# Recommendation kernel: a tile's gathers split by partitions, a token of three tiles fetched row by row, seven token buffers

## The chip, the cores and the metric

The kernel runs on one core of a Trainium2 chip. The metric is device time in microseconds of that core; lower is better. Before the change the median of three runs is 7685.06 us (7660.61 to 7702.07).

## The reference

A batch of 16384 examples goes through embedding look-ups and a small network:

```python
tok = word_emb[token_idx].mean(axis=1)          # 32 tokens of 300 values, table of 50000 rows
e1, e2, e3 = means of 20 rows of 64 values each, tables of 1000, 5000 and 10000 rows
o1, o2, o3, o4 = one row of 64 values each, tables of 100, 50, 20 and 1000 rows
emb = concatenate([tok, e1, e2, e3, o1, o2, o3, o4], axis=1)       # 748 values
wide = sums of the same look-ups in tables of one column
h = relu(emb @ W1 + b1); h = relu(h @ W2 + b2); h = relu(h @ W3 + b3)   # 1024, 512, 256
return sigmoid(h @ Wd + bd + wide)
```

All of it is in float32. The 32 token look-ups are far the largest part of the data: 16384 x 32 rows of 1200 bytes, 629 MB.

## The kernel before

The batch is cut into 128 tiles of 128 examples, one example per partition. Indices come in blocks of four tiles (`load_indices`, L266), the network runs on blocks of two tiles, 256 examples (`mlp`, L474).

Each tile goes through two separate paths.

- The small tables stay on the chip. For each tile VectorE makes one-hot rows (`one_hots`, L322), TensorE multiplies them into counts (`counts`, L340), ScalarE evicts the counts from the one `pc` buffer (L347), and TensorE multiplies counts by table rows (`small_sums`, L365). This is done in 11 steps to a tile.
- The 32 token rows of each example are gathered from HBM by GpSimd (`tokens`, L245): one indirect DMA per token and tile, 128 rows of 1200 bytes each (L255), 4096 in all. Two tokens make a group with one buffer, `tok_rows`; there are 16 groups to a tile and eight buffers (`TOK_BUFS`). VectorE adds a group into a running sum in PSUM (`add_up`, L237 to L243) three groups after its gathers were issued in the program's order (`TOK_LAG`). A gather waits for the add that read its buffer eight groups before.

Then both are transposed (L405 to L431) and the network follows: matmuls in `layer` (L461), evictions with relu by ScalarE (L470), the last sum (L490), the sigmoid (L491) and the store of 256 results by SyncE (L493). The tiles `h1` and `h3` of the network have one buffer between them: the first eviction of the next block overwrites what the store reads.

The order of the work is written out by hand. One loop of 1424 steps (L570; 128 tiles of 11 steps and 16 more) issues for each step its one-hots and counts, then as many token groups as keep pace with the steps (`toks.to`, L608: 2051 calls over 1424 steps), then small sums, then matmuls of the network. `Paced` (L496) runs a generator until it has done a given amount. Each engine works through its own instructions in this order. GpSimd's queue holds little but gathers. SyncE's queue holds the loads of indices, tables and weights, and the stores; each transfer that SyncE issues uses one of eight semaphores in turn, and waits for the transfer before on that semaphore.

Of the kernel before, what the change touches and what calls it, by code (L numbers as in the profile page):

```python
# [8 lines left out]
F32 = mybir.dt.float32  # L9
BF16 = mybir.dt.bfloat16  # L10
FP8 = mybir.dt.float8e3
I32 = mybir.dt.int32
U32 = mybir.dt.uint32
# [4 lines left out]
P = 128  # L18
N_TOK, TOK_D = 32, 300
# [2 lines left out]
D1, D2, D3 = 1024, 512, 256  # L22
TOK_GROUP = 2
TOK_LAG = 3
TOK_BUFS = 8
WAKE = 16
EARLY = 3
BLOCK = 512
# [6 lines left out]
STEPS = -(-HALF // ONEHOT)  # L35
# [3 lines left out]

SMALL = ("o4", "e1", "e2", "e3", "o1", "o2", "o3")
WIDE_IN_FRONT = ("mh1", "mh3", "oh2")
G_COLS = 7 * ROW
# [7 lines left out]
def kernel(  # L52
# [21 lines left out]
    nc = tc.nc  # L74
    B = out.shape[0]
    NSUB, N = BLOCK // P, LAYER_TILES * P
# [4 lines left out]
    slices, n_h = {}, 0  # L81
    for f in SMALL:
        n = -(-tables[f].shape[0] // P)
        slices[f] = (n_h, n_h + n)
        n_h += n

    tokp = ctx.enter_context(tc.tile_pool(name="tok", bufs=TOK_BUFS))
    const = ctx.enter_context(tc.tile_pool(name="const", bufs=1))
    idxp = ctx.enter_context(tc.tile_pool(name="idx", bufs=3))
    keyp = ctx.enter_context(tc.tile_pool(name="keys", bufs=1))  # L90
    scp = ctx.enter_context(tc.tile_pool(name="sc", bufs=2))
    ohp = ctx.enter_context(tc.tile_pool(name="onehot", bufs=2))
# [74 lines left out]
    def convert_tables():  # L167


        tags = ("even", "odd")  # L170
        parts = range(0, n_h, PART)
        raws = [load_tables(parts[k], tags[k]) for k in range(2)]
        yield
        pieces = []
        for k, part0 in enumerate(parts):
            for at in range(part0, min(part0 + PART, n_h), SPLIT):
                pieces.append((k, at, min(at + SPLIT, part0 + PART, n_h)))

        def term(p, c):
            _, a, b = pieces[p]  # L180
            return terms[:, a:b, c * ROW : (c + 1) * ROW]

        def rows(p):
            k, a, b = pieces[p]
            return raws[k][:, a - parts[k] : b - parts[k], :]

        def make(p, c):

            if c == 0:
                nc.scalar.activation(term(p, 0), rows(p), AF.Copy, scale=2.0)  # L190
                return
            _, a, b = pieces[p]
            left = ps_h.tile([P, SPLIT, ROW], F32, name="left", tag="ph")[:, 0 : b - a, :]
            nc.tensor.matmul(left, ident, rows(p), start=True, stop=False)  # L194
            for k in range(c):
                nc.tensor.matmul(left, minus_half, term(p, k), start=False, stop=(k == c - 1))
            nc.scalar.activation(term(p, c), left, AF.Copy, scale=2.0)

        for step in range(len(pieces) + 2):
            for c in (2, 1, 0):  # L200
                if 0 <= step - c < len(pieces):
                    make(step - c, c)
            k, _, b = pieces[min(max(step - 2, 0), len(pieces) - 1)]
            if step >= 2 and b in parts and k + 2 < len(parts):
                raws.append(load_tables(parts[k + 2], tags[k % 2]))
            yield 1
# [10 lines left out]
    def load_weights():  # L217
        for k, rows in enumerate(chunk_rows):
            at = 0
            for a, b in rows:  # L220
                nc.sync.dma_start(out=w1_sb[at : at + b - a, k, :], in_=w1[a:b, :])
                at += b - a
        nc.sync.dma_start(out=w2_sb, in_=w2.rearrange("(k p) m -> p k m", p=P))
        nc.sync.dma_start(out=w3_sb, in_=w3.rearrange("(k p) m -> p k m", p=P))
        for sb, dram in ((wd_sb, wd), (b1_sb, b1), (b2_sb, b2), (b3_sb, b3), (bd_sb, bd)):
            nc.sync.dma_start(out=sb, in_=dram)
# [5 lines left out]

    def add_up(t, q, rows):

        a, b = rows[:, 0:TOK_D], rows[:, TOK_D : 2 * TOK_D]
        if q == 0:
            nc.vector.tensor_add(tok_sum, a, b)  # L237
        else:
            nc.vector.tensor_add(tok_sum, tok_sum, a)  # L239
            to = tok_sum  # L240
            if q == n_groups - 1:
                to = sums_of[t] = gp.tile([P, TOK_D], F32, name="g_tok")
            nc.vector.tensor_add(to, tok_sum, b)  # L243

    def tokens():  # L245

        under_way = []
        for n in range(n_all):
            if n < n_all - TOK_LAG:
                t, q = divmod(n, n_groups)  # L250
                it = token_indices[t // NSUB][:, t % NSUB, :].bitcast(U32)
                rows = tokp.tile([P, TOK_GROUP * TOK_D], F32, name="tok_rows")
                for r in range(TOK_GROUP):
                    j = q * TOK_GROUP + r
                    nc.gpsimd.indirect_dma_start(  # L255
                        out=rows[:, r * TOK_D : (r + 1) * TOK_D],
                        out_offset=None,
                        in_=word,
                        in_offset=bass.IndirectOffsetOnAxis(ap=it[:, j : j + 1], axis=0),
                    )  # L260
                under_way.append((t, q, rows))
            if n >= TOK_LAG:
                add_up(*under_way.pop(0))
            yield 1

    def load_indices(blk):  # L266


        b0 = blk * BLOCK
        it = idxp.tile([P, NSUB, N_TOK], I32, name="it")  # L270
        nc.sync.dma_start(
            out=it, in_=idx[b0 : b0 + BLOCK, 0:N_TOK].rearrange("(s p) c -> p s c", p=P)
        )
        ix = keyp.tile([P, NSUB // 2, 2, N_SMALL], I32, name="ix")
        for s in range(NSUB):
            nc.sync.dma_start(
                out=ix[(s % 2) * HALF : (s % 2 + 1) * HALF, s // 2],
                in_=idx[b0 + s * P : b0 + (s + 1) * P, IDX_MH:IDX_COLS].rearrange(
                    "(f p) c -> p f c", p=HALF
                ),  # L280
            )
        token_indices[blk] = it
        return ix

# [276 lines left out]
    ctx.enter_context(tc.manual_schedule())  # L561
    ix = load_indices(0)
    toks = Paced(tokens())
    tables_on_chip = convert_tables()
    next(tables_on_chip)
    tables_on_chip = Paced(tables_on_chip)
# [3 lines left out]
    for step in range(n_steps):  # L570
        t, i = divmod(step, STEPS)
        s = t % NSUB
        if i == 0:
            if g is not None:
                wide_term(g)
                waiting.append((step + 1, Block.add_small, t - 2, g))
            sums = g = None
            if 1 <= t <= tiles:
                g = gp.tile([P, G_COLS], F32, name="g")
                sums = sums_by_step(small_sums(g, cnt))  # L580
            if t < tiles:
                if s == 0 and t:
                    sc = next_sc
                cnt = cp.tile([P, 2, HALF, n_h], FP8, name="cnt", tag="counts")
        if t < tiles:
            hot_now = hot
            if s == 1 and i == 0 and t + NSUB < tiles:
                ix = load_indices(t // NSUB + 1)
            if s == 2 and i == 0 and t + NSUB < tiles + 1:
                next_keys = lookup_keys(ix)  # L590
            if i < STEPS - 1:
                hot = one_hots(sc, s, i + 1)
            elif t + 1 < tiles:
                hot = one_hots(next_sc if s == NSUB - 1 else sc, (s + 1) % NSUB, 0)
            counts(cnt, hot_now, i)
            tables_on_chip.to(TABLE_PACE * (step - 2))
            if t == 1 and i == STEPS - 1:
                load_weights()
        if waiting and step >= waiting[0][0]:
            block = transpose(*waiting.pop(0)[1:])  # L600
            if block:
                if layers:
                    layers.finish()
                layers = Paced(mlp(block), LAYER_TIME * block.n / P)
                last = block.first + block.n // P
                begin, left = step, min(ready(ends[last] - 1) if last < tiles else n_steps, n_steps - EARLY) - step
        known = set(sums_of)
        toks.to(n_all * (step + 1) / n_steps)  # L608
        for k in set(sums_of) - known:
            waiting.append((step + 2, Block.add_tokens, k, sums_of.pop(k)))  # L610
        if s == 2 and i == 1 and t + NSUB < tiles + 1:
            next_sc = key_columns(next_keys)
        ahead = 0
        if sums:
            done = next(sums)
            ahead = n_h * (i + 1) / STEPS - done
        if layers:
            layers.to(mlp_work * layers.size * (step + 1 - begin) / left + ahead)
        if step == n_steps - EARLY:
            part = early_part(block_of[tiles - 1])  # L620
# [43 lines left out]
```

## Time and profile before

| What | Value |
|---|---|
| Median of the three runs | 7685.06 us |
| Span of the profiled execution, first to last instruction | 5191.3 us |
| Own time of the profiled execution | not given by the page; its span lies 2493.8 us below the runs' median |
| Granted clock of TensorE, mean | 0.998 |
| TensorE busy | 5113.7 us (99%) |
| VectorE busy | 3890.9 us (75%) |
| ScalarE busy | 2600.7 us (50%) |
| GpSimd busy | 3888.4 us (75%) |
| Queue of the gathers | 629.41 MB, 44.2% of 16 DMA engines |
| Read from HBM | 645.59 MB, 124 GB/s over the span |

The span is counted in one execution under the profiler. Busy times count what an engine computes or, for GpSimd, the making of a gather's descriptors; issuing a transfer on SyncE or ScalarE and waiting for semaphores are not counted. A line such as `L255 POOL DMA_INDIRECT` names the source line, the engine and the operation, then what it writes and reads. In a list of waits the numbers are microseconds in total, how often, and the longest. In a timeline they are the start, the duration, and, in brackets, how long the engine sat idle before and what ended it. `SPq` is SyncE's queue.

### The profile page before, as it was taken

To read this page: it belongs to the slowest core of one execution; us is meant where nothing else is said; L and a number is where in the kernel's file an instruction comes from. 1 tells how busy PE (TensorE), PEld (TensorE's weight loads), DVE (VectorE), ACT (ScalarE), POOL (GpSimd) and SP (SyncE) were. 2 spreads that over 40 slices of the span, in tenths; PEclk is the share of its full clock that TensorE was granted. 3 is DMA by queue.
4 is the path that set the end of the run, shared out by engine and by line. 5 is a ranking of instruction groups with operands and counts; after the bars stand their busy time and mean duration, and the time that the engine had idled before them with its cause. 6 is when DMAs were issued, how large, how long until landed. Compare 5 with 4: busy or idle time off the path is not lost.

```text
span 5191.3 us, 116518 instructions
## 1 busy us (share of the span) xinstructions
PE 5113.7 (99%) x46912; PEld 4177.5 (80%) x46912; DVE 3890.9 (75%) x8502; ACT 2600.7 (50%) x2445; POOL 3888.4 (75%) x4103
## 2 busy tenths in 40 slices
PE   7999999999999999999999999999999999999999
PEld 5888888888888888888888888888888878888888
DVE  6777777777777777777777777777777777777773
ACT  6555555555545545545445455555555545555552
POOL 7777777777777777777777777777777777777774
PEclk9999999999999999999999999999999999999999
DMA  7444444444444444444444444444444444444442
GB/s 201 123 126 125 125 126 124 125 126 125 126 124 126 125 126 125 126 124 126 125 126 126 124 126 125 126 126 123 125 125 126 125 126 124 126 125 126 124 124 77
DMA packets 253019, 653.38 MB, mean 126 GB/s; under 512 B 119056, under 2 KB 119633, under 8 KB 252477
## 3 DMA queue, kind: packets, MB, share of 16 engines
q0 software_dynamic: 196608, 629.41, 44.2%
q1 hardware_dynamic: 55869, 16.53, 1.4%
q8 instruction: 367, 6.01, 0.5%
q14 instruction: 175, 1.43, 0.1%
HBM read 645.59 MB, written 0.07 MB: 124 GB/s over the span
## 4 chain that ended last, share of the span: by engine, by line
PE 94%; DVE 2%; issue 1%; DMA 1%; ACT 0%; POOL 0%; SPq 0%; DVEq 0%; ACTq 0%
PE ph L461 46%; PE pg L365 32%; PE pc L340 12%; PE po L486 1%; PE pt L426 1%; PE pt L410 1%; PE pt L407 1%; DMA tok_rows<-in_word_emb_dram,it 1%; DVE own L239 1%; DVE own L243 0%; DMA w_sb<-in_W_dram 0%; POOL tok_rows L255 0%; DVE slice L322 0%; PE left L194 0%; PE pt L427 0%
## 5 line engine op out<-in xcount | busy, mean ns | idle before, releaser
L255 POOL DMA_INDIRECT tok_rows<-in_word_emb_dram,it x4096 | 3887.5, 949 | 1260.5 <-issue 873.6
L347 ACT ACTIVATE cnt<-pc 128x1656 fp8e3<-128x1656 f32 (+1 forms) x1408 | 2124.6, 1509 | 1607.7 <-PE pc L340 1592.1
L365 PE MATMUL pg<-terms,cnt 128*128 128x195 bf16 x17664 | 1828.7, 253 | 7.9 <-DVE g L371 7.6
L365 PEld LDWEIGHTS <-cnt 128*128 128x128 fp8e3 x17664 | 1590.3, 144 | 162.1 <-issue 31.8
L461 PE MATMUL ph<-h,w_sb 128*128 128x256 f32 (+1 forms) x5200 | 1224.2, 379 | 0.5 <-ACT h L470 0.5
L461 PE MATMUL ph<-x_small,w_sb 128*128 128x256 f32 (+2 forms) x4128 | 1044.4, 381 | 4.8 <-DVE x_small L429 3.0
L461 PEld LDWEIGHTS ph<-h,w_sb 128*128 128x128 f32 x5200 | 930.8, 191 | 99.2 <-issue 0.8
L322 DVE TENSOR_TENSOR row<-own,sc 128x768 bf16<-128x768 bf16 (+1 forms) x1408 | 762.3, 541 | 304.2 <-PE pc L340 251.5
L239 DVE TENSOR_TENSOR own<-own,tok_rows 128x300 f32<-128x300 f32 x1920 | 917.0, 478 | 63.3
L243 DVE TENSOR_TENSOR own<-own,tok_rows 128x300 f32<-128x300 f32 x1792 | 856.8, 478 | 61.8
L340 PEld LDWEIGHTS <-row 64*128 64x128 bf16 x16384 | 495.4, 94 | 484.8 <-issue 227.5
L470 ACT ACTIVATE h<-ph,b_sb 128x256 f32<-128x256 f32 (+1 forms) x906 | 426.8, 471 | 912.3 <-PE ph L461 912.0
L461 PEld LDWEIGHTS ph<-x_small,w_sb 128*128 128x128 f32 (+1 forms) x4128 | 739.3, 191 | 86.6 <-PE ph L461 6.4
L322 DVE TENSOR_TENSOR slice<-own,sc 128x828 bf16<-128x828 bf16 (+1 forms) x1408 | 795.5, 565 | 0.0
L340 PE MATMUL pc<-slice,row 64*128 64x138 bf16 x16384 | 751.0, 223 | 15.8 <-DVE slice L322 9.0
L461 PE MATMUL ph<-x_tok,w_sb 128*128 128x256 f32 (+1 forms) x2064 | 565.4, 380 | 0.0
L371 DVE TENSOR_REDUCE g<-pg 128x130 f32<-128x390 f32 (+1 forms) x512 | 261.1, 510 | 393.6 <-PE pg L365 391.0
L461 PEld LDWEIGHTS ph<-x_tok,w_sb 128*128 128x128 f32 x2064 | 373.0, 192 | 40.9
L428 DVE TENSOR_SCALAR x_tok<-pt 128x256 f32<-128x256 f32 x128 | 54.4, 425 | 301.6 <-PE pt L427 301.6
L411 DVE TENSOR_TENSOR x_small<-pt,scale 128x384 f32<-128x384 f32 x128 | 71.2, 556 | 91.8 <-PE pt L410 91.8
L486 PE MATMUL po<-h,wd_sb 128*1 128x256 f32 (+1 forms) x260 | 68.0, 374 | 1.6 <-DVE x_small L429 1.0
L490 DVE TENSOR_TENSOR h<-po,wide_row 1x256 f32<-1x256 f32 (+1 forms) x65 | 26.5, 408 | 54.9 <-PE po L486 51.9
(55 smaller groups left out, 872.4 us busy)
## 6 DMA issues: line engine op xcount, KB each, us to landing
tok_rows<-in_word_emb_dram,it POOLq DMA_INDIRECT x4096
ix<-in_idx_dram SPq DMA_DIRECT2D x128, 32.0 KB
w_sb<-in_W_dram SPq DMA_DIRECT2D x6, 512.0 KB
raw<-in_mh_dram SPq DMA_DIRECT2D x4, 682.5 KB
it<-in_idx_dram SPq DMA_DIRECT2D x32, 64.0 KB
w_sb<-in_W_dram SPq DMA_DIRECT2D x1, 2048.0 KB
out_dram<-h SPq DMA_DIRECT2D x63, 1.0 KB
raw<-in_mh_dram SPq DMA_DIRECT2D x2, 227.5 KB
```

The lines of the kernel that those rows point to most:

```text
L239: nc.vector.tensor_add(tok_sum, tok_sum, a)
L243: nc.vector.tensor_add(to, tok_sum, b)
L255: nc.gpsimd.indirect_dma_start(out=rows[:, r * TOK_D : (r + 1) * TOK_D], out_offset=None, in_=word, in_offset=bass.IndirectOffsetOnAxis(ap ...
L322: nc.vector.tensor_tensor(one[:, 0:rows, :].rearrange("p i (n d) -> p i n d", d=2), iota[:, 0:n].rearrange("p (n d) -> p n d", d=2).unsque ...
L340: nc.tensor.matmul(pc[:, f, k // n, at : at + n_h], hot[0][half, k, :], hot[1][half, k, :], start=True, stop=True,)
L347: nc.scalar.activation(cnt[:, :, b : b + rows, :].rearrange("l f (g k) h -> l f g (k h)", g=2), pc[:, :, :, 0 : n * n_h], AF.Copy, scale=0 ...
L365: nc.tensor.matmul(pg[:, j, :], by_slice[:, :, h], terms[:, h, :], start=(h == h0), stop=(h == h1 - 1))
L371: nc.vector.tensor_reduce(g[:, at : at + n * ROW].rearrange("p (f d) -> p f d", f=n), pg[:, 0:n, :].rearrange("p f (c d) -> p f d c", c=3) ...
L411: nc.vector.tensor_tensor(self.small[:, 0:3, at], pt[:, 0:3, :], scale.unsqueeze(2).to_broadcast([P, 3, P]), ALU.mult)
L461: nc.tensor.matmul(ph[:, 0:n], weights[: src.shape[0], k, m * P : (m + 1) * P], src, start=(k == 0), stop=(k == len(srcs) - 1),)
L470: nc.scalar.activation(dst[:, m, 0:n], ph[:, 0:n], AF.Relu, bias=bias[:, m : m + 1])
L486: nc.tensor.matmul(po[:, 0:n], wd_sb[:, k : k + 1], h3[:, k, 0:n], start=(k == 0), stop=(k == M3 - 1))
```

## The change

Three things are changed, and the loop of steps gets one call more.

- In tile 18 nine of the 32 gathers, those of tokens 4, 6, ... 20, become two each, by partitions (`PARTS`): 64 and 64 rows, 96 and 32, 112 and 16, 120 and 8, 124 and 4, 126 and 2, 125 and 3, 127 and 2 (row 126 is in both), 32 and 96. The indices of each second part are loaded once more by SyncE, so that they begin at partition 0 (`load_lower`).
- In tiles 30, 40 and 50 the last token isn't gathered. Its 128 indices are loaded as a row on one partition; registers are loaded from it, 16 at a time; and each of the 128 rows of the table is moved by a transfer of its own, whose address comes from a register. SyncE issues them, but for the first 32 rows of tile 40, which ScalarE issues. They go five to a step, from step 275, 385 and 495 (`FETCH_FROM`, and the last `yield` of `fetch_rows`). The three tiles use one buffer.
- There are seven token buffers in place of eight. `add_up` gets the two halves of a group as two operands, since the second may lie in the buffer of the fetched rows.

```diff
-TOK_BUFS = 8
+TOK_BUFS = 7
...
+FULL = ((0, 128),)
+PARTED = (18,)
+PARTS = {
+    4: ((0, 64), (64, 128)),
+    6: ((0, 96), (96, 128)),
+    8: ((0, 112), (112, 128)),
+    10: ((0, 120), (120, 128)),
+    12: ((0, 124), (124, 128)),
+    14: ((0, 126), (126, 128)),
+    16: ((0, 125), (125, 128)),
+    18: ((0, 127), (126, 128)),
+    20: ((0, 32), (32, 128)),
+}
+FETCHED = {30: 0, 40: 32, 50: 0}
+FETCH_FROM = 25
...
+    lowp = ctx.enter_context(tc.tile_pool(name="lower", bufs=1))
...
-        a, b = rows[:, 0:TOK_D], rows[:, TOK_D : 2 * TOK_D]
+        a, b = rows
...
-                rows = tokp.tile([P, TOK_GROUP * TOK_D], F32, name="tok_rows")
+                tok_rows = tokp.tile([P, TOK_GROUP * TOK_D], F32, name="tok_rows")
+                rows = []
                 for r in range(TOK_GROUP):
                     j = q * TOK_GROUP + r
-                    nc.gpsimd.indirect_dma_start(
-                        out=rows[:, r * TOK_D : (r + 1) * TOK_D],
-                        out_offset=None,
-                        in_=word,
-                        in_offset=bass.IndirectOffsetOnAxis(ap=it[:, j : j + 1], axis=0),
-                    )
+                    if j == N_TOK - 1 and t in FETCHED:
+                        rows.append(fetched.pop(t))
+                        continue
+                    rows.append(tok_rows[:, r * TOK_D : (r + 1) * TOK_D])
+                    for a, b in PARTS.get(j, FULL) if t in PARTED else FULL:
+                        index = it[a:b, j : j + 1] if a == 0 else lower[t, a][:, j : j + 1].bitcast(U32)
+                        nc.gpsimd.indirect_dma_start(
+                            out=rows[-1][a:b],
+                            out_offset=None,
+                            in_=word,
+                            in_offset=bass.IndirectOffsetOnAxis(ap=index, axis=0),
+                        )
...
+    def fetch_rows():
+        for t, n_scalar in FETCHED.items():
+            rows = fetched[t] = lowp.tile([P, TOK_D], F32, name="fetched")
+            column = lowp.tile([1, P], I32, name="column")
+            nc.sync.dma_start(
+                out=column, in_=idx[t * P : (t + 1) * P, N_TOK - 1 : N_TOK].rearrange("n o -> o n")
+            )
+            for p0 in range(0, P, 16):
+                queue, engine = nc.sync, mybir.EngineType.SP
+                if p0 < n_scalar:
+                    queue, engine = nc.scalar, mybir.EngineType.Activation
+                _, values = nc.values_load_multi_w_load_instructions(
+                    column[:, p0 : p0 + 16],
+                    engines=[engine],
+                    min_val=0,
+                    max_val=word.shape[0] - 1,
+                    skip_runtime_bounds_check_because="the indices are rows of the table",
+                )
+                for i, value in enumerate(values):
+                    p = p0 + i
+                    queue.dma_start(out=rows[p : p + 1, :], in_=word[bass.ds(value, 1), :])
+                    yield 1
+            yield (10 * STEPS - 26) * 5 + 2
+
+    def load_lower(t):
+        b0 = t * P
+        for a in sorted({a for parts in PARTS.values() for a, _ in parts if a}):
+            part = lower[t, a] = lowp.tile([P, N_TOK], I32, name="lower", tag=f"lower{a}")[0 : P - a, :]
+            nc.sync.dma_start(out=part, in_=idx[b0 + a : b0 + P, 0:N_TOK])
...
+        for t in PARTED:
+            if t // NSUB == blk:
+                load_lower(t)
...
+    fetches = Paced(fetch_rows())
...
+        fetches.to(5 * (step - FETCH_FROM * STEPS))
```

More of the change, by code (lines that the diff above doesn't have):

```diff
@@ L264, in tokens @@
             yield 1
+    lower, fetched = {}, {}
+    def fetch_rows():
[26 more added lines that the diff above has]
+            nc.sync.dma_start(out=part, in_=idx[b0 + a : b0 + P, 0:N_TOK])
     def load_indices(blk):
```

## The prediction

> **What bounds the kernel now.** I read the page first (busy shares, chain, groups), then the waits of GpSimd, VectorE and SyncE, then timelines of single engines. First the shares and the chain by engine:
>
> ```profile
> PE 5113.7 (99%) x46912; PEld 4177.5 (80%) x46912; DVE 3890.9 (75%) x8502; ACT 2600.7 (50%) x2445; POOL 3888.4 (75%) x4103
> ...
> PE 94%; DVE 2%; issue 1%; DMA 1%; ACT 0%; POOL 0%; SPq 0%; DVEq 0%; ACTq 0%
> ```
>
> TensorE is busy for 5113.7 of 5191.3 us and holds 94% of the chain. GpSimd's 75% deceives: the gathers' group, their line by itself and GpSimd's waits show why.
>
> ```profile
> L255 POOL DMA_INDIRECT tok_rows<-in_word_emb_dram,it x4096 | 3887.5, 949 | 1260.5 <-issue 873.6
> ```
>
> ```profile
> L255 POOL DMA_INDIRECT tok_rows<-in_word_emb_dram,it x4096: 942/949/1323, 3.1 to 5148.6; - x196
> ```
>
> ```profile
> POOL tok_rows L255 <- issue: 873.6, 2866, 0.3
> ...
> POOL tok_rows L255 <- DVE own L243: 92.0, 267, 7.7
> ```
>
> Each gather takes 949 ns, and ahead of nearly each stand 0.3 us in which nothing is waited for. (3887.5 + 1260.5)/4096 = 1.257 us a gather; the typical distance is 1.254, and 4096 x 1.254 = 5136 us, the whole span. In the trace only three gaps exceed 0.33 us: 1.5 at 87 us, 2.3 at 5107, 7.7 at 5126, each a wait for a buffer. So GpSimd has no idle time to give.
>
> Does it pace TensorE? A step (5191.3 us/1424 = 3.646 us) takes 2051/1424 groups of two gathers, so a group has 3.646/1.440 = 2.531 us against the gathers' 2 x 1.254 = 2.508. In mid-span, 22 steps take 79.5 us, which is 2.508 us a group: the two are level. VectorE's waits say which leads:
>
> ```profile
> DVE row L322 <- PE pc L340: 251.5, 270, 3.1
> ...
> DVE low L289 <- DMA ix<-in_idx_dram: 3.6, 1, 3.6
> ```
>
> VectorE waits for TensorE, and its list has no wait for a gather. TensorE leads. But the cushion is thin: pairing the last packet of each gather with its add, the least distance is 1.0 to 1.4 us up to 1000 us, 0.6 near 1300 to 1800, and 5 or more after 2500 (where TensorE lost some 6 us by itself). What makes the gathers late by more than about a microsecond before 2000 us is passed on.
>
> SyncE, by its waits, the store's line, and its timeline:
>
> ```profile
> SPq L493 <- ACT h L491: 4966.7, 65, 111.9
> ```
>
> ```profile
> L493 SPq DMA_DIRECT2D out_dram<-h x65: 224/233/270, 211.0 to 5189.3; - x65
> ```
>
> ```profile
> 1958.87 80.51 SPq L493 DMA_DIRECT2D out_dram<-h  x2
> 2039.69 0.40 SPq L271 DMA_DIRECT2D it<-in_idx_dram  x1
> 2040.31 2.75 SPq L276 DMA_DIRECT2D ix<-in_idx_dram  x4
> ```
>
> Nearly all of its time is waiting for the sigmoid (L491) ahead of a store, one store per 79.5 us; what is put into its queue between two stores runs in that window. Past the window it delays the store, and this has a taker: the next block's h1 lies in the buffer that the store reads. ScalarE's timeline:
>
> ```profile
> 1004.54 0.51 ACT L491 ACTIVATE h<-h,bd_sb 1x256 f32<-1x256 f32 x1 [0.56 <-DVE h L490]
> 1007.22 1.55 ACT L347 ACTIVATE cnt<-pc 128x1656 fp8e3<-128x1656 f32 x1 [2.18 <-PE pc L340]
> 1010.05 0.47 ACT L470 ACTIVATE h<-ph,b_sb 128x256 f32<-128x256 f32 x1 [1.27 <-PE ph L461]
> ```
>
> The store is issued at 1005.07, its packets end 1.4 us later; the eviction that overwrites the buffer starts at 1010.05. So a store may come about 3.4 us late for nothing; after that ScalarE, and with it TensorE, stands.
>
> **What the Trainium skill says.** "DMA: Bandwidth & Descriptors", section "Why a DMA increments its semaphore by 16 and not by 1": the number of DMA engines is the largest up to 16 that divides the slowest dimension; it names 127 partitions as one engine, with an exception for some GpSimd copies. The trace has only 128-row gathers (48 packets each), so it shows neither. The same page, "Anatomy of one DMA — SWDGE (gpsimd) path": a wait stands on the issuing sequencer, so what is behind it in that queue waits too. L493's 4966.7 us agree. "Perfetto Trace Analysis", "Sequencer Loop": an engine instruction is queued and the sequencer goes on; so ScalarE can issue transfers while an ACTIVATE runs. No row shows it, since ScalarE issues none.
>
> **The change part by part.** The changed kernel's order has the same TensorE and VectorE instructions in the same order. So nothing gets shorter on the bound; all that can be added is waiting.
>
> *Nine split gathers* (tile 18, about 725 to 765 us): nine more gathers. If a gather's 949 ns are all row work, each extra costs its 0.306 us gap, 2.8 in all; if all fixed, 1.254, so 11.3. I take the middle, 7.0. The pair of token 18 (rows 0 to 127, 126 to 128) writes row 126 twice, so the second waits for the first to land: 1.58 us after a gather's end in the packets, less the 0.3 gap: 1.3. GpSimd is 8.3 us later. If the 127 rows go to one DMA engine: a packet of four rows takes 276 ns, so 32 packets take 8.8 us there in place of two in 0.6 us: 8 more. The exception would make it 0, which I take, keeping 8 as the end.
>
> *Seven buffers*: a gather then waits for the add seven groups back. In the first 260 us that distance is -3.4 us at its least: GpSimd comes out some 3.7 us later behind the stall at 87 us. Later (2600 to 3500 us) it is -2.2, where the gathers have 5 us or more to spare: 0.
>
> Together GpSimd is 12.0 us late at 770 us. Off go 1.4 (cushion of the adds there) and 1.5 (VectorE is about that far ahead of TensorE's next one-hots; between 0 and 3): about 9 us onto TensorE, once, because the two go at one pace afterwards. Ends: 3.7 + 2.8 + 1.3 - 1.4 - 3 = 3 and 3.7 + 11.3 + 1.3 + 8 - 1 = 23.
>
> *Three gathers gone* (tiles 30, 40, 50): GpSimd gains 3 x 1.254 = 3.8 us at 1200, 1600 and 2000 us. TensorE leads and doesn't run faster for it: 0, at most -3.8.
>
> *352 rows by SyncE.* Five per step: 110 in a window, with seven register loads of 16 indices. A row: issue 0.26 (between the store's 0.233 and the 0.287 of the 1x1 bd_sb load), 0.11 for its address and the gap (waits in SP's queue stand 0.06 apart), and the register load, which no row shows: the skill's "Runtime: NRT & Kernel Launch", "Instruction fetch mechanics", has about 200 ns a register. 0.57 us; 110 rows make 63 us. The window holds 79.5 + 3.4 = 83, so the limit is 0.75 us a row. Cost 0; cover 20 us. Dear end: an issue as slow as ix (0.607) makes 0.92 us, 101 us, 18 late. Eight are in flight, each waiting for the one eight back; landing as the store does, 1.4 us after its issue, they set no limit. Queued behind them: stores (above), and index loads, needed a tile (40 us) later.
>
> *32 rows by ScalarE* (tile 40, near 1400 us, 6.4 steps): 5 x 0.37 = 1.9 us of its sequencer per 3.65 us step, next to 50% busy, that is 1.8 idle; what doesn't fit goes under a running ACTIVATE. The two register loads (0.6 to 3.2 us each) delay an eviction, and with one pc buffer TensorE waits: I take 4 us, ends 0 and 18.
>
> *Eight small index loads and three columns* by SyncE: about 0.3 us each in windows with room, 0.
>
> Sum: 9 + 4 = 13 us, span 5204. The page gives no time of the profiled execution itself; the runs' median lies 7685.06 - 5191.3 = 2493.8 us above its span. What fills that no view shows. I leave it constant: 7685 + 13 = 7698.
>
> **The rivals.**
> *SyncE late (slower).* From 0.75 us a row the store is late. For: the issue with a computed address and the register load have no row here. Against: 0.57 has a margin of a quarter. At 1.0 us: tiles 30 and 50 lose 110 - 83 = 27 each; tile 40 (87 rows and 2.8 us of index loads) 7: 61 us, 7685 + 13 + 61 = 7759.
> *All of it hidden.* VectorE's cushion takes the late gathers, and ScalarE's 50% the rows: 7685. For: VectorE is 75% busy. Against: it gains nothing on GpSimd, whose pace is TensorE's.
> *What lies around the span goes with the transfers.* Some 4350 are issued now, about 400 more after: 400/4350 x 2494 = 229 us, 7914. For: its cause is unknown. Against: as well the inputs' size, which stays.
>
> **How the numbers follow.** A measurement of this kernel can tell about 0.5% (38 us) from no change. The sum: 0.66, own range 7665 to 7735; SyncE late 0.17; hidden 0.13; around the span 0.04. Low end 7660, the lowest run of before, since nothing can be gained; high end 7765, SyncE late at 1.0 us with some scatter. Slower: 0.17 + 0.04 + 0.03 from the sum's dear ends; faster 0.03, scatter alone.
>
> **What would show it.** Split gathers' durations (0.95 each, or in proportion to rows); 1.3 us ahead of the second of the 127 pair; a new wait of VectorE for gathers, of a few us, after 730 us; SyncE's rows at about 0.57 us and its wait at L493 still tens of us in those windows; ScalarE's h without a long wait for a store. Wrong if SyncE's rows fill their windows, or if span and time move apart.

## The result and the profile after

The changed kernel takes 7708.23 us (median of 18 runs, 7689.01 to 7727.34); the kernel before, on the same chip, takes 7685.92 us (18 runs, 7660.61 to 7710.85). The medians differ by 22 us. The ratio worked out from all the runs is 1.0031, interval [1.0021, 1.0042]: 24 us more, between 16 and 32. (Here and below, ratios and the us that follow from them are of this kind, so they can differ by some us from the difference of the medians.) That is less than the 38 us which the prediction took for no change, but the interval leaves zero out.

The profiled execution of the changed kernel has its own time, 7717.23 us, and a span of 7715.1 us. So only 2.1 us lie around the span: the 2493.8 us that the prediction left "around the span" were no part of the execution whose span it read. In the page, the lines that answer to those shown of before (shares, TensorE's granted clock, chain by engine, gathers):

```profile
PE 6014.3 (78%) x46912; PEld 4726.7 (61%) x46912; DVE 3890.3 (50%) x8502; ACT 2576.7 (33%) x2445; POOL 3885.0 (50%) x4109
...
PEclk8888888888888888888888888898888888888889
...
PE 52%; another core or an unknown queue 19%; DVE 13%; issue 11%; ACT 5%; DMA 1%; DVEq 0%; SPq 0%; ACTq 0%
...
L278 POOL DMA_INDIRECT tok_rows<-in_word_emb_dram,it x4093 | 3876.1, 947 | 3774.9 <-DVE own L259 2449.9
```

Read the clock row first. TensorE had its full clock in the execution whose profile was shown before (mean 0.998), and a mean of 0.873 here: it goes back and forth between full and half. All 18 runs of the changed kernel lie at 0.87 as well. TensorE is busy 6014 us in place of 5114 for the same 46912 matmuls, and has 22% of idle time besides. With the kernel before, executions with a clock near 1.00 take 5194 us, and those near 0.87 take 7554 us on one chip. On the chip of this result, where it takes 7686 us, its own clock is not on record, only the changed kernel's. So only runs of one chip are compared in what follows.

The engines around TensorE then look different, by the waits of GpSimd and VectorE and by that of SyncE (total us, times, longest):

```profile
POOL tok_rows L278 <- DVE own L259: 2449.9, 684, 16.5
...
DVE row L383 <- remote: 1394.5, 238, 9.0
...
DVE own L255 <- DMA tok_rows<-in_word_emb_dram,lower: 2.5, 2, 1.7
DVE own L259 <- DMA tok_rows<-in_word_emb_dram,it: 2.2, 2, 1.3
```

```profile
SPq L554 <- ACT h L552: 6825.7, 62, 178.0
```

GpSimd, which before had no idle time to give, now waits 2450 us for VectorE to free buffers. "remote" is a releaser that the profile doesn't name, but the trace's record of semaphores shows it: all 829 such waits of ScalarE and VectorE are for TensorE's own semaphore, which comes a median 3.8 us, and at most 10.9 us, after the recorded end of the last matmul that raises it. The traces at full clock have no such wait. Whether TensorE still computes until then or stands can't be told, since the ends of matmuls are modelled. The only waits of an add for a gather come to 4.7 us, and all of them stand in tile 18. SyncE waits for the sigmoid as before, so its rows do not make the stores late.

Where is the 24 us? The evictions of counts (L408) cut the run into tiles of 11. Windows of two tiles: 16 and 17, then 18 and 19, then 20 and 21 (columns: length, busy time and count of each engine, granted clock, DMA share, GB/s):

```profile
979.35:1096.67 117.32, 88.68 (x726) 71.40 (x725) 59.75 (x133) 39.66 (x37) 58.95 (x63) 0.88 0.30 81
1096.67:1235.93 139.26, 99.37 (x752) 77.41 (x751) 62.72 (x135) 39.74 (x37) 74.08 (x77) 0.82 0.29 79
1235.93:1356.08 120.15, 93.58 (x724) 73.44 (x724) 60.22 (x133) 39.89 (x37) 58.60 (x62) 0.86 0.30 80
```

The window with the nine split gathers takes 139.3 us, its neighbours 117.3 and 120.2: 20 us more, with the lowest clock of the three. Single tiles scatter by 3.4 us at this clock (standard deviation), so one window is an indication and no proof. GpSimd's timeline in it (start, duration, then idle before and releaser), then ScalarE's and TensorE's:

```profile
1136.18 2.54 POOL L278 DMA_INDIRECT tok_rows<-in_word_emb_dram,it  x1 [3.32 <-DVE own L259]
1147.03 0.87 POOL L278 DMA_INDIRECT tok_rows<-in_word_emb_dram,lower  x1 [8.31 <-DMA tok_rows<-in_word_emb_dram,it]
```

```profile
1168.97 1.55 ACT L408 ACTIVATE cnt<-pc 128x1656 fp8e3<-128x1656 f32 x1 [15.80 <-remote]
```

```profile
1170.58 0.87 PE L401 MATMUL pc<-slice,row 64*128 64x138 bf16 x12 [12.55 <-ACT cnt L408]
```

"To make" a gather means here GpSimd's busy time for it. The gather of 127 rows takes 2.54 us to make, the next stands 8.31 us until it has landed, and 33 us after the start of the first end the longest wait of ScalarE and the longest pause of TensorE in the whole trace, 15.80 and 12.55 us. No gather ends that pause: the last add that waited for one runs at 1154.80 us, and ScalarE, which TensorE waits for, stood for TensorE's late semaphore. So the pause follows the split, and the way from one to the other doesn't show. GpSimd also waited 3.32 us for a buffer just before, so part of its lateness had cover.

### The profile page after: what moved, and what is told of

Its sections match the earlier page's. It is cut to its first block, busy times and chain, and to the rows that moved or that the text cites. A ratio compares the mean times of both kernels' runs of the same rounds, so it can differ in the third digit from the quotient of the medians.

```text
span 7715.1 us, 117733 instructions
## 1 busy us (share of the span) xinstructions
PE 6014.3 (78%) x46912; PEld 4726.7 (61%) x46912; DVE 3890.3 (50%) x8502; ACT 2576.7 (33%) x2445; POOL 3885.0 (50%) x4109
## 3 DMA queue, kind: packets, MB, share of 16 engines
q14 instruction: 184, 1.51, 0.1%
## 4 chain that ended last, share of the span: by engine, by line
PE 52%; another core or an unknown queue 19%; DVE 13%; issue 11%; ACT 5%; DMA 1%; DVEq 0%; SPq 0%; ACTq 0%
PE ph L522 23%; PE pg L426 17%; PE pc L401 8%; ACT cnt L408 4%; DVE own L255 4%; DVE slice L383 3%; DVE own L259 3%; PE po L547 1%; DVE row L383 1%; PE pt L471 1%; ACT h L531 1%; PE pt L487 1%; DMA tok_rows<-in_word_emb_dram,it 1%; PE left L210 0%
## 5 line engine op out<-in xcount | busy, mean ns | idle before, releaser
L408 ACT ACTIVATE cnt<-pc 128x1656 fp8e3<-128x1656 f32 (+1 forms) x1408 | 2122.5, 1507 | 3249.6 <-remote 1652.1
L426 PE MATMUL pg<-terms,cnt 128*128 128x195 bf16 x17664 | 2193.7, 274 | 449.9 <-issue 399.8
L426 PEld LDWEIGHTS <-cnt 128*128 128x128 fp8e3 x17664 | 1820.0, 147 | 723.2 <-issue 605.8
L401 PE MATMUL pc<-slice,row 64*128 64x138 bf16 x16384 | 823.4, 236 | 865.7 <-ACT cnt L408 364.5
L522 PE MATMUL ph<-h,w_sb 128*128 128x256 f32 (+1 forms) x5200 | 1387.7, 409 | 95.3 <-issue 86.1
L401 PEld LDWEIGHTS <-row 64*128 64x128 bf16 x16384 | 574.6, 100 | 1370.4 <-issue 1208.8
L522 PE MATMUL ph<-x_small,w_sb 128*128 128x256 f32 (+2 forms) x4128 | 1196.1, 418 | 90.2 <-issue 70.8
L522 PEld LDWEIGHTS ph<-h,w_sb 128*128 128x128 f32 x5200 | 1017.6, 209 | 274.0 <-issue 142.5
L522 PEld LDWEIGHTS ph<-x_small,w_sb 128*128 128x128 f32 (+1 forms) x4128 | 823.8, 213 | 236.4 <-issue 120.5
L432 DVE TENSOR_REDUCE g<-pg 128x130 f32<-128x390 f32 (+1 forms) x512 | 261.3, 510 | 1260.3 <-remote 548.7
L522 PE MATMUL ph<-x_tok,w_sb 128*128 128x256 f32 (+1 forms) x2064 | 617.3, 406 | 17.4 <-issue 16.5
L472 DVE TENSOR_TENSOR x_small<-pt,scale 128x384 f32<-128x384 f32 x128 | 70.9, 554 | 120.2 <-PE pt L471 90.7
L471 PE MATMUL pt<-ident,g 128*128 128x128 f32 x384 | 79.9, 326 | 3.4 <-issue 3.3
```

What stands on the lines that cost most here:

```text
L401: nc.tensor.matmul(pc[:, f, k // n, at : at + n_h], hot[0][half, k, :], hot[1][half, k, :], start=True, stop=True,)
L408: nc.scalar.activation(cnt[:, :, b : b + rows, :].rearrange("l f (g k) h -> l f g (k h)", g=2), pc[:, :, :, 0 : n * n_h], AF.Copy, scale=0 ...
L426: nc.tensor.matmul(pg[:, j, :], by_slice[:, :, h], terms[:, h, :], start=(h == h0), stop=(h == h1 - 1))
L432: nc.vector.tensor_reduce(g[:, at : at + n * ROW].rearrange("p (f d) -> p f d", f=n), pg[:, 0:n, :].rearrange("p f (c d) -> p f d c", c=3) ...
L471: nc.tensor.transpose(pt[:, k, :], g[:, c : c + P], ident)
L522: nc.tensor.matmul(ph[:, 0:n], weights[: src.shape[0], k, m * P : (m + 1) * P], src, start=(k == 0), stop=(k == len(srcs) - 1),)
```

## The experiments

**Theory**: the nine split gathers cost the time, since GpSimd, level with TensorE, is late by each extra gather and by the wait inside token 18's pair; the rest costs nothing. **Rivals**: the rows by SyncE or ScalarE cost it; the seven buffers do. The first eight kernels ran where the kernel before takes 5194 us, that is, at a clock near 1.00; four more at 0.87.

### Fourteen split tiles, nothing else

```diff
-TOK_BUFS = 7
-PARTED = (18,)
-FETCHED = {30: 0, 40: 32, 50: 0}
+TOK_BUFS = 8
+PARTED = tuple(range(18, 126, 8))
+FETCHED = {}
```

> The nine split gathers alone, in 14 tiles (18, 26, ... 122) instead of one, eight token buffers, no rows fetched. If the splits are the whole of the change's 22 us, 14 x 22 = 308 us more than before (ratio 1.040). If they cost only the 4.7 us that VectorE waits for the 127-row gather and its neighbours in the trace of the changed kernel, 14 x 4.7 = 66 us (1.009). If GpSimd's waits for buffers (2449.9 us there) cover them, nothing (1.000).

Measured: 5469.38 against 5193.99 us, ratio 1.0529 [1.0515, 1.0543]: 275 us, 19.7 a tile. In the waits, VectorE's adds, which waited for no gather before, now lead VectorE's list (GpSimd's wait inside token 18's pair is the third line):

```profile
DVE own L259 <- DMA tok_rows<-in_word_emb_dram,it: 340.2, 469, 2.8
...
DVE own L255 <- DMA tok_rows<-in_word_emb_dram,lower: 215.7, 73, 11.2
...
POOL tok_rows L278 <- DMA tok_rows<-in_word_emb_dram,it: 149.6, 116, 9.1
```

```profile
L278 POOL DMA_INDIRECT tok_rows<-in_word_emb_dram,lower x126 | 111.5, 885 | 152.6 <-DMA tok_rows<-in_word_emb_dram,it 118.5 <-issue 31.1 <-DMA tok_rows<-in_word_emb_dram,lower 3.1
```

The group is that of the 126 second parts, of 2 to 96 rows: 885 ns each on the mean, against 949 for a whole gather. So most of a gather's making doesn't go with its rows. With the 0.30 us ahead of each, an extra gather is 1.19 us, nine are 10.7. Some first parts are dearer than a whole gather, those of 124, 125 and 127 rows above all. With them, all gathers of a split tile take 40.4 us to make, against 30.3 in another tile; the nine gaps of 0.31 us make it 12.9 us more for GpSimd, before any waiting. The eight small index loads go with the splits in every run here; with fourteen times as many, SyncE still waits 4928.0 us for the sigmoid, against 4966.7 before, so they don't make its stores late.

### 1408 rows by SyncE

```diff
-PARTED = (18,)
-FETCHED = {30: 0, 40: 32, 50: 0}
-FETCH_FROM = 25
+PARTED = ()
+FETCHED = {t: 0 for t in range(20, 121, 10)}
+FETCH_FROM = 15
```

> The last token of 11 tiles (20, 30, ... 120) by rows of SyncE alone, 1408 rows instead of 352, no splits, seven buffers. In the trace of the changed kernel 110 rows take 78.9 us of a window of some 124 us between two stores, so the store isn't late: 0 us (1.000) beside what seven buffers cost. If SyncE's rows are the whole of the 22 us, four times as much, 88 us (1.011).

Measured: 5194.89 us, ratio 1.0002 [0.9993, 1.001]. Eleven tiles' rows, 1408 of them, cost nothing. The lines of the transfers and of the register loads by themselves (ns, least/median/most):

```profile
L313 SPq FUSED_REGOPS  x1408: 37/37/51, 531.9 to 4653.8; - x176
L313 SPq MOVE fetched<-in_word_emb_dram x1408: 29/29/38, 532.0 to 4653.9; - x176
L313 SPq DMA_DIRECT2D fetched<-in_word_emb_dram x1408: 219/225/299, 532.1 to 4653.9; - x176
```

```profile
L304 SPq TENSOR_LOAD <-column x88: 1142/1232/1397, 530.7 to 4646.4; - x88
```

An issue with a computed address takes 225 ns, its two register operations 66, a load of 16 registers 1232, 77 to a row. In the timeline of the changed kernel at this clock 110 rows take 54.6 us, 0.50 each, of a window of 80. The limit of 0.75 is far.

### The same rows by ScalarE

Against the kernel of the section above:

```diff
-FETCHED = {t: 0 for t in range(20, 121, 10)}
+FETCHED = {t: 128 for t in range(20, 121, 10)}
```

> The same 11 tiles, but all 128 rows of each by ScalarE, 1408 rows instead of 32, no splits, seven buffers. By the prediction's 4 us for 32 rows, 44 x 4 = 176 us (1.023). If ScalarE's rows are the whole of the 22 us, 44 x 22 = 968 us (1.126). If they fit beside its work, which leaves two thirds of its time free, 0 us (1.000).

Measured: 5206.11 us, ratio 1.0023 [1.0013, 1.0032]: 12 us (7 to 17) for 1408 rows; by their share, an estimate, 0.3 us for the change's 32. Of the 1408 issues 963 start while an ACTIVATE runs, as the prediction expected. ScalarE's waits:

```profile
ACT h L531 <- DMA fetched<-in_word_emb_dram: 92.3, 67, 2.7
```

Evictions of the network stand behind the rows' transfers 67 times, up to 2.7 us, 92 us in all. About a tenth of that reaches the end of the run.

### Seven buffers alone

```diff
-TOK_BUFS = 8
+TOK_BUFS = 7
```

in the kernel before.

> The kernel before with seven token buffers, nothing else. The prediction had GpSimd late by 3.7 us for it, of which less reaches TensorE: at most 1.0005. GpSimd waits for buffers anyway in the trace of the changed kernel, so 1.000. If the buffers are the whole of the 22 us, 1.003.

Measured: 5194.2 us, ratio 1.0000 [0.9992, 1.0009]: nothing, within 5 us either way. In its trace GpSimd's stall near 88 us is 2.91 us in place of 1.51. So GpSimd is 1.4 us late there and not 3.7, and at 720 us it is level with the kernel before.

### The change as it is, and without its splits

The changed kernel, unedited, on a chip at full clock; and

```diff
-PARTED = (18,)
+PARTED = ()
```

> The changed kernel itself. Theory A (the split tile makes the gathers late, and the lateness is handed on whole): where the kernel before takes 5194 us, what one of the 14 tiles cost, 19.7 us, and 0.3 us for ScalarE's rows: +20 us (1.0038). Where it takes 7685 us: +22 us (1.003) again. Theory B (the prediction's sum): +13 us (1.0025 at 5194, 1.0017 at 7685).

> The changed kernel with tile 18 gathered as before; the fetched rows and the seven buffers stay. Theory A: no more than 1 us over the kernel before where that takes 5194 us (1.000). Where it takes 7685 us, also 1.000 if the splits are the cause there; 1.003 if the rows or the buffers are. Theory B: 4 us for ScalarE's rows (1.0008).

Measured against 5194.1 us: as changed 5212.48, ratio 1.0035 [1.0021, 1.0048], 18 us; without splits 5194.89, ratio 1.0001 [0.9992, 1.0009]. At full clock the splits are the whole of it, as far as the interval of the kernel without them can tell (-4 to +5 us). GpSimd's timeline in tile 18 of the kernel as changed, from the 124-row gather on:

```profile
748.35 1.28 POOL L278 DMA_INDIRECT tok_rows<-in_word_emb_dram,it  x1 [0.30 <-DMA tok_rows<-in_word_emb_dram,lower]
749.93 0.89 POOL L278 DMA_INDIRECT tok_rows<-in_word_emb_dram,lower  x1 [0.30 <-issue]
...
756.12 1.19 POOL L278 DMA_INDIRECT tok_rows<-in_word_emb_dram,it  x1 [0.30 <-issue]
...
760.08 2.54 POOL L278 DMA_INDIRECT tok_rows<-in_word_emb_dram,it  x1 [0.30 <-issue]
770.75 0.87 POOL L278 DMA_INDIRECT tok_rows<-in_word_emb_dram,lower  x1 [8.13 <-DMA tok_rows<-in_word_emb_dram,it]
```

The line at 760.08 is the 127-row gather; the next begins only when it has landed. 0.30 us of the 8.13 stand before any gather, so the wait proper is 7.8. In a DMA view of 765 to 769 us, in which that gather is the only one under way (packets, MB, the queue's share of 16 engines):

```profile
q0 software_dynamic: 40, 0.10, 6.7%
```

6.7% of sixteen engines is 1.07 engines: the 127 rows go on one. VectorE and TensorE then:

```profile
772.92 0.48 DVE L255 TENSOR_TENSOR own<-own,tok_rows 128x300 f32<-128x300 f32 x1 [8.62 <-DMA tok_rows<-in_word_emb_dram,lower]
```

```profile
779.28 2.77 PE L426 MATMUL pg<-terms,cnt 128*128 128x195 bf16 x16 [12.15 <-DVE g L432]
```

The add waits 8.6 us, the work behind it in VectorE's queue with it, and TensorE pauses 12.15 us, until `g` (L432), which stands behind that add, is done. Here the way from the gather to TensorE shows step by step. The pause of 12.55 us in the execution at 0.87 is nearly as long, but it was not ended in this way.

### Which half of the splits

Two variants of the fourteen split tiles change token 18 alone, in `PARTS`: the two rows before the 127, so that the wait falls on a short transfer, and 112 and 16 rows in place of 127 and 2.

```diff
-    18: ((0, 127), (126, 128)),
+    18: ((126, 128), (0, 127)),
...
-    18: ((0, 127), (126, 128)),
+    18: ((0, 112), (112, 128)),
```

> The nine splits in 14 tiles, eight buffers, no rows fetched, as measured at +275 us; but of token 18's pair the two rows go first and the 127 rows second, so that GpSimd no longer stands 8.2 us for the landing of the 127 rows. If that standing is what costs: per tile 8 x 1.2 + 1.2 + 1.6 + 1.3 - 1 = 13, 14 x 13 = 180 us at 5194 (1.035). If the late landing itself costs (VectorE needs the 127 rows whoever waits), nearly as before: 14 x 18 to 19 = 260 us (1.050).

> The nine splits in 14 tiles as measured at +275 us, but token 18 is cut into 112 and 16 rows instead of 127 and 2. If the 127 rows go to one DMA engine and cost 8.2 us of landing and 1.6 us of making, what is left is nine more gathers of 1.2 us: 10.8 less about 1 of cushion, 14 x 9.8 = 137 us at 5194 (1.026). If the number of gathers is all, as before: 275 us (1.053).

Measured against 5194.1 us: two rows first 5382.58, ratio 1.0363 [1.0349, 1.0377], 188.5 us or 13.5 a tile; 112 rows 5331.36, ratio 1.0264 [1.025, 1.0278], 137.3 us or 9.8 a tile. Timelines of the first variant, GpSimd and then VectorE:

```profile
758.44 0.87 POOL L278 DMA_INDIRECT tok_rows<-in_word_emb_dram,lower  x1 [0.30 <-issue]
760.86 2.55 POOL L278 DMA_INDIRECT tok_rows<-in_word_emb_dram,it  x1 [1.55 <-DMA tok_rows<-in_word_emb_dram,lower]
```

```profile
771.68 0.48 DVE L255 TENSOR_TENSOR own<-own,tok_rows 128x300 f32<-128x300 f32 x1 [9.26 <-DMA tok_rows<-in_word_emb_dram,it]
```

This tells two things apart. Here VectorE waits as long for the 127 rows (9.26 us) as in the changed kernel, but GpSimd stands 1.55 us in place of 8.13 and goes on gathering into free buffers; and 6.2 of the 19.7 us a tile are gone. So at full clock what costs is mainly GpSimd standing, since nothing makes its gathers up; a late landing by itself is mostly caught up.

The sum per tile, from these traces: with 112 rows a split tile takes GpSimd 38.8 us to make, which with the nine gaps is 11.3 us more than another tile, and 9.8 are measured. The 1.5 us between them are put down to the cushion; no run measures it by itself. Two rows first: 11.3 + (2.55 - 0.92 for making 127 rows rather than 112) + (1.55 - 0.30) - 1.5 = 12.7; measured 13.5. As in the change: 11.3 + 1.6 + 7.8 - 1.5 = 19.2; measured 19.7.

### The same at a clock of 0.87

Four kernels ran on a chip where the kernel before takes 7554.24 us at a clock of 0.87 to 0.88: the one without splits, the fourteen split tiles, the change as it is, and the change with 112 and 16 rows for token 18. Only the last is a new edit:

```diff
-    18: ((0, 127), (126, 128)),
+    18: ((0, 112), (112, 128)),
```

> The changed kernel with tile 18 whole, once more, in the hope of a chip on which the kernel before takes 7685 us (TensorE at a granted clock near 0.87) and not 5194 us. If the nine splits of tile 18 are what costs 22 us there too: within 5 us of the kernel before. If on such a chip it is the row transfers or the seven buffers instead: 22 us slower. On a chip where the kernel before takes 5194 us both theories expect within 2 us of it, as measured already.

> Fourteen tiles split, eight buffers, no row transfers, once more, for a chip on which the kernel before takes 7685 us. If GpSimd paces the kernel's split tiles there as well (they cost 20 us a tile on a 5194 us chip): +280 us. If TensorE's slower clock gives GpSimd room between the stalls (its gathers then have 3.77 us a group on the mean, against 2.51 of work), part of each tile's 20 us is covered: +100 to +200 us. On a 5194 us chip +275 us.

> The changed kernel itself beside the two others on the same chip: +22 us if the kernel before takes 7685 us there, +18 us if it takes 5194 us.

> The changed kernel with token 18 of tile 18 cut into 112 and 16 rows, in place of 127 and 2. If the standing GpSimd is what counts, and half of it is the gather of 127 rows on one DMA engine, as the fourteen tiles showed: +9 to +10 us on a 5194 us chip (18 less the 9 to 10 that this gather costs), +10 to +13 on a 7685 us chip. If the nine extra gathers make the whole of it in a single tile: still +18.

| Kernel | us, median | Ratio | us over before |
|---|---|---|---|
| no splits | 7575.90 | 1.0036 [1.0014, 1.0057] | 27 (11 to 43) |
| fourteen split tiles | 7804.16 | 1.0319 [1.0293, 1.0345] | 241 (221 to 261) |
| as changed | 7599.65 | 1.0059 [1.004, 1.0078] | 45 (30 to 59) |
| as changed, 112 rows | 7594.56 | 1.0056 [1.0035, 1.0077] | 42 (26 to 58) |

Fourteen tiles: 17.2 us each. That is between the two expectations (280 without cover, 100 to 200 with it), so little is covered in spite of GpSimd's long waits elsewhere. Within this one trace, the windows of two tiles that begin with a split one take 134.8 us on the mean, and the others 115.9, with a standard deviation of 3.7: 19 us a tile. So a split tile costs at this clock nearly what it costs at full clock. But it doesn't cost it in the same way, by all that the waits show:

```profile
DVE own L259 <- DMA tok_rows<-in_word_emb_dram,it: 0.3, 1, 0.3
...
DVE own L255 <- DMA tok_rows<-in_word_emb_dram,lower: 0.2, 1, 0.2
```

All adds together wait 0.5 us for gathers, where the same kernel at full clock has the hundreds of us shown above. What is longer in the split tiles is the wait for TensorE's late semaphore. The nine longest waits of ScalarE, 15.4 to 22.4 us, all but one of this kind, end 33 to 41 us after the start of a gather of 127 rows; the longest other one is 12.7 us. How the gather leads to them is not shown.

The windows of tiles 18 and 19, first without splits, then as changed, then with 112 rows:

```profile
1068.12:1190.54 122.42, 96.11 (x753) 75.29 (x752) 62.78 (x136) 39.48 (x37) 64.19 (x68) 0.89 0.33 89
```

```profile
1063.78:1200.70 136.92, 98.22 (x753) 76.57 (x752) 62.77 (x136) 39.70 (x38) 74.38 (x77) 0.83 0.30 80
```

```profile
1073.88:1207.22 133.34, 100.89 (x753) 78.09 (x752) 62.86 (x135) 39.66 (x37) 72.54 (x77) 0.82 0.30 81
```

With the splits the window is 14.5 us longer and its clock 0.83 in place of 0.89; with 112 rows it is 10.9 longer. In each of the three traces with one split tile this window is the longest of the sixty from tile 4 to tile 123, 17 to 21 us over the mean of the others. "As changed" stands 24 us over "no splits" by the medians, 14 by the means.

Three expectations missed. "No splits" was to lie within 5 us of the kernel before if the splits are the cause, and 22 over it if the rows or the buffers are. It lies 22 over by the medians, 27 by the ratio, with an interval that leaves zero out: taken alone, what the rival foresaw. "As changed" was expected 22 us over and is 45; with 112 rows it was expected at 10 to 13, or 18, and is 42. In the trace of "no splits" SyncE still waits 6697.9 us for the sigmoid, so late stores don't make the 27 us. No add waits for a gather either, but the fourteen split tiles cost 241 us with hardly such a wait, so that clears nothing. Whether the rows or the seven buffers cost here was not run apart. The gain of 112 rows (3 us of 45) is lost in intervals of 15 us either way: inconclusive.

## Why the prediction was right

Forecast 7698, measured 7708, and the order of cases was right: a small loss, SyncE not late, nothing going with the number of transfers. Part of it was luck. The terms were read from an execution at full clock, and only at full clock do the traces show the way that the prediction described. The measured execution ran at 0.87, where GpSimd is not level with TensorE but waits 2450 us; that the splits cost about as much there was not foreseen by any step of the prediction. And at full clock two terms missed in opposite directions.

- **TensorE leads, GpSimd level with it, a thin cushion.** Right at full clock. Of 20.7 us of lateness (12.9 of making and gaps, 7.8 of standing) 19.7 a tile reached TensorE in the fourteen tiles, and 18.4 in the single one. So 1.0 to 2.3 were taken off, where the prediction put 1.4 and 1.5 together. At 0.87 "GpSimd has no idle time to give" doesn't hold.
- **Nine extra gathers, 7.0 us.** Mis-sized: 10.7, and 11.3 with the dearer first parts. The choice of the middle between "all row work" and "all fixed" failed; the cost is fixed to nine tenths, near the dear end of 11.3.
- **The 127 rows: "the exception would make it 0, which I take, keeping 8 as the end".** This choice failed. The Trainium skill, "DMA: Bandwidth & Descriptors", section "Why a DMA increments its semaphore by 16 and not by 1", names 127 partitions as one engine, and the 6.7% share agrees: the gather does not have the exception of some direct copies. In place of 1.3 us it cost 1.6 of making and 7.8 of standing: 9.4, the 9.3 of the prediction's own dear end.
- **Seven buffers, 3.7 us late.** Mis-sized: 1.4 us late at full clock, gone by 720 us, and no cost, within 5 us either way.
- **Together 12.0 us late, 9 onto TensorE.** 12.9 + 7.8 = 20.7 late, 18 to 20 onto TensorE, at full clock.
- **Three gathers gone: 0.** Not tried alone; the kernel without splits, which has it together with the rows and buffers, shows no gain (1.0001).
- **SyncE's rows, 0.57 us each, hidden.** Right: 0.50. The register load was priced too dear at about 200 ns a register, by the Trainium skill, "Runtime: NRT & Kernel Launch", section "Instruction fetch mechanics"; measured 77.
- **ScalarE's 32 rows, 4 us.** Mis-sized: 0.3, by their share of the 12 us for 1408. The rows do delay evictions, as it said, but some nine tenths of the delay is hidden.
- **Sum 13.** At full clock 18, from 9 turned to 18 and 4 turned to 0. Two terms missed in opposite directions, which is why the total was close.
- **"What lies around the span", 2493.8 us, constant.** Wrong in kind. The span of one execution was compared with the median of others that ran at another clock. Had the shown span's clock (0.998) been doubted against the runs, the same sum would have had to be argued for an execution with half-clock stretches and waiting gathers. The rival built on it, 7914, had no ground. The prediction's own sign of being wrong, "if span and time move apart", came true for this reason: the span that it read and the one shown after differ by 2524 us, the times by 22.

Of the result's 24 us (16 to 32), one split tile at 17.2 leaves 7, give or take 8. Against that stands the 27 (11 to 43) of the kernel without splits on another chip at the same clock. So at a clock of 0.87 the splits are shown to be a cost, of 17 to 21 us a tile by fourteen tiles and by the windows; how it comes about there, and whether the rows and buffers add something, stays open. At full clock the way is shown, and rows and buffers add nothing that could be measured.

## What to carry to other kernels

Where gathers are level with the bound engine, count instructions and not rows: cutting a gather in two costs nearly a whole gather, and a second gather that must wait for the first to land costs that landing on the whole GpSimd queue, while the same landing awaited by VectorE alone is mostly made up. Long waits of GpSimd are no proof that such a cut is free: at 0.87 it cost as much. Choose the number of partitions with care: 127 rows ran on a single DMA engine, and the next gather stood 7.8 us for them. And before a span is set beside a median, compare the clock of both: a gap of a third between them was not something around the kernel here, it was another execution.

## What the runs showed of the hardware

- **The making of a gather depends on how its rows divide.** In tile 18 64, 96 and 112 rows take 0.91 to 0.93 us, 120 and 126 about 0.98, 125 take 1.19, 124 take 1.28 and 127 take 2.54. By the skill's rule for the number of DMA engines (the section named above) these are 16 engines for the first three, then 15, 14, 5, 4 and 1, an estimate but for the 127 rows, which the trace shows on one. It isn't the number of engines that counts, since second parts of 2, 3 and 4 rows, by the same rule on as many engines, take only 0.87 to 0.89. It is the rows to an engine: 0.86 us and 0.013 for each row of one engine, fitted to these figures, give all of them within 0.04 us, from 1 row (0.87) over 25 and 31 (1.19 and 1.28) to 127 (2.54). That the one follows from the other was not tried by itself.
- **Half clock comes with TensorE's pauses.** The Trainium skill, "TensorE: Matmul & The Clock Gate", section "HAM oscillation — how this bites in real kernels", says that a pause over about 3.4 us lowers TensorE's clock. In the change at full clock, the window before tile 18 and the window with it:

```profile
650.00:730.00 80.00, 78.86 (x731) 64.55 (x730) 62.18 (x139) 40.00 (x37) 60.50 (x65) 1.00 0.47 124
720.00:800.00 80.00, 64.40 (x567) 52.17 (x567) 46.16 (x103) 30.28 (x30) 55.10 (x57) 0.89 0.37 95
```

  The mean of 0.89 comes from 17 us at half clock in two stretches. One, 760.0 to 763.4 us, follows a pause of only 2.31 us, shorter than the page's figure. The other, 770.2 to 783.9, begins inside the pause of 12.15 us and outlasts it by 4.6 us. So only 8 of the 17 us fell on work. The mean clock of the whole run falls with the pauses: 0.998 before, 0.990 to 0.993 with 112 rows in fourteen tiles, 0.984 with two rows first, 0.979 with the splits as they are. At full clock this needs no term of its own, since the sum by GpSimd's lateness leaves less than a microsecond a tile. At 0.87 the window of the splits has its lower clock and its longer time together; which of the two causes the other there was not tried.
- **Chips or executions differ by half.** The same kernel takes 5194 us at a clock near 1.00 and 7554 us near 0.87. Half-rate stretches alone do not fill that gap: in the changed kernel at 0.87 TensorE is busy 900 us longer than in the kernel before at full clock, and idle some 1620 us longer (7715 - 6014 against 5191 - 5114). Of its 1700 us of idle time 1059 lie inside the waits for TensorE's own semaphore, which no trace at full clock has. So much of what is counted as idle is TensorE reporting late. What brings a chip into this was not found.
